# Edge attention over degree-sorted node tiles: the 53-node tile goes first and its free lanes take edges of the fullest nodes

## The chip, the core and the metric

The kernel runs on one core of a Trainium2 chip. Times are device microseconds of one execution, the median of several runs. A profile is one further execution, recorded instruction by instruction; its span runs from the first to the last instruction of the program. The core has engines with queues of their own: PE (matrix products and transposes, PEld its weight loads), DVE (element-wise work and reductions), ACT (functions and copies), POOL (here mostly the issue of indirect transfers) and SP (the issue of plain transfers).

## The reference

A graph of N = 3125 nodes with 256 features and E = 100000 edges, sorted by target, passes through two layers. The parts that the change touches are three passes of attention over edges: two transformer convolutions in layer 0 (4 heads of 64) and one attention with edge features in layer 1 (8 heads of 32).

```python
# layer 0, twice
qi, kj, vj = (q[dst], k[src], v[src])
alpha = jnp.sum(qi * kj, axis=-1) / math.sqrt(out_ch)
amax = jax.lax.stop_gradient(jax.ops.segment_max(alpha, dst, num_segments=n))
ex = jnp.exp(alpha - amax[dst])
denom = jax.ops.segment_sum(ex, dst, num_segments=n)
alpha = ex / denom[dst]
out = jax.ops.segment_sum(vj * alpha[..., None], dst, num_segments=n)
...
return out + x @ ws + bs
# layer 1
e = (edge_attr @ We.T).reshape(-1, HEADS, OUT_CH)
k_e = k[src] + e
v_e = v[src] + e
alpha = jnp.einsum('ehc,ehc->eh', q[dst], k_e) / jnp.sqrt(jnp.float32(OUT_CH))
...
```

In layer 1 alpha goes through the same softmax over the edges of a target, the weights multiply v_e, the products are summed per target, and a skip term x @ Wskip is added.

A convolution is followed by a batch norm over the nodes and a leaky ReLU. Beside them layer 0 has four blocks of a linear-attention mixer over all nodes and a routed feed-forward (16 experts, 2 per node); layer 1 has a second mixer and a feed-forward over selected nodes. The results are added to x.

## The kernel before

**Tiles of nodes.** node_order (L729) sorts the nodes by in-degree on the chip. From the sorted targets it finds each node's first edge and its number of edges, ranks the nodes by falling degree, and puts rank r into tile r // 128, lane r % 128. There are 25 tiles; 24 are full, and the last one holds the 53 nodes of least degree, with 75 lanes free. SLOTS (L715) gives each tile a fixed number of slots, one per edge of a lane: 64 for the first, then 43, 41 and so on down to 22; the sum is 833. Of the order, `perm` holds the node of a lane (free lanes get row numbers past the table's end), `near` the same limited to N - 1, `base` the lane's first edge, `lo` and `hi` the slots that hold real edges, and `some` whether the lane has any. If a tile's nodes have more edges than slots, a flag (`over`) makes the program run a general version after this one. With the reference's inputs the fullest node has 55 edges.

**Slots and steps.** `fill` (L915) gathers the source nodes of a tile's slots and makes a bias of 0 or -BIG per slot. `steps` (L1031) cuts a tile's slots into subs of at most 8 and puts two subs into a step: 64 slots are four steps of 8 + 8, 43 are 8 + 7, 7 + 7, 7 + 7, and 22 are 8 + 7 and 7. All tiles have 63 steps in a pass.

**One step.** SlotOrder (L1052) issues for each slot one indirect transfer (L723, called from L1081) that brings 128 rows of 2 KB, key and value of the source node of each lane. Then come, for each sub, the multiply of keys by q (L1103) and the sum over a head (L1106); for the step, bias and maximum (L1116 to L1120), exponential (L1131) and its sum (L1138); for each sub the multiply of values (L1144) and the sum over slots by transposes that accumulate on PE (L216). ACT takes the sum out (L1163), PE turns it back (L230), and ACT keeps it as one part of `res` (`kept`, L1171). In layer 1, EdgeOrder (L1288) adds the projected edge features to keys and values first: a transfer of the lane's edge attributes, transposes (L1320), products (L1336), and adds on DVE (L1347).

**Joining the parts.** A tile has two to four parts, one a step, each with a maximum `mx`, a sum `den` and a result `res`. `join_max` (M in PATTERN, L1049 and L1292) runs in the tile's last step and turns the maxima into factors; `join_sum` (N) into shares; `join` (J, L1202, multiply at L1206) runs in the first step of the next tile and scales `res` in place; `output` (O, U) adds the parts up on PE (L1594 or L2834), adds the skip term, and stores the tile. The tiles of mx, den and res come from pools with two buffers.

**The order of work.** PATTERN is the order in which the pieces of a step are issued to PE, DVE and ACT; these three queues follow the program (manual_schedule). At each `m` in it, a share of another stage's work is put in: the four mixer blocks of layer 0 during the two convolutions (Filling, L940), the mixer of layer 1 during the third pass (Mixing, L997). The share is the total of that work by the number of points, which counts the steps (L1537, L2851). The order on POOL and SP is not written out; the framework's scheduler sets it, and both work in order. The buffers of the gathered rows are four subs, so POOL can be one step ahead.

**Between passes.** `stages(i)` brings the tile's node features (from a table by `near` in the first convolution and in layer 1, from the stored `hsp` in the second, L1558), turns them and makes q. `output` of a convolution also takes the batch statistics of the tile's real nodes (L1614). After each convolution the stored tiles are normalised, multiplied or turned, and written by `perm` to the rows of a table (put_rows, L1038).

Of the kernel before, what the change touches and what calls it, by code (L numbers as in the profile page):

```python
# [10 lines left out]
F32 = mybir.dt.float32  # L11
# [3 lines left out]
ALU = mybir.AluOpType  # L15
AX = mybir.AxisListType
# [3 lines left out]
P = 125  # L20
# [661 lines left out]
def l0_gnn(k, x, conv, y_mix, xcur):  # L682
# [31 lines left out]

SLOTS = [  # L715
    64, 43, 41, 39, 38, 37, 36, 35, 35, 34, 33, 33, 32, 32, 31, 30, 30, 29, 29, 28, 27, 26, 25, 24, 22
# [12 lines left out]
def node_order(k, dram, src, dst, keep, tmp, pp, over, loads, weights):  # L729
# [5 lines left out]
    NQ, NB = len(SLOTS), max(SLOTS)  # L735
    assert N <= NQ * 128
# [113 lines left out]
    count = nc.vector.tensor_reduce(rank, pos, axis=AX.X, op=ALU.add)  # L850
# [18 lines left out]
    for c, t in enumerate((node[:, :NT], first[:, :NT], num)):  # L869
# [8 lines left out]
    own = one.tile([128, NQ], F32, name="own")  # L878
    nc.gpsimd.memset(past, 0.0)
    nc.gpsimd.iota(  # L880
        own, pattern=[[128, NQ]], base=0, channel_multiplier=1, allow_small_or_imprecise_dtypes=True
    )
    nc.vector.scalar_tensor_tensor(past[:, :, 0], own, N - 0.5, own, op0=ALU.is_gt, op1=ALU.mult)
    caps = one.tile([128, NQ], F32, name="caps")
    for i in range(NQ):
        nc.gpsimd.memset(caps[:, i : i + 1], float(SLOTS[i]))
    ps = pp.tile([128, 512], F32, name="cps", tag="cps")
# [12 lines left out]

    bf = one.tile([128, NQ], F32, name="bf")
# [3 lines left out]
    nc.vector.tensor_copy(perm, pl[:, :, 0])  # L905
    nc.vector.tensor_scalar_min(near, pl[:, :, 0], N - 1.0)
# [3 lines left out]
    nc.vector.tensor_tensor(more, pl[:, :, 2], caps, op=ALU.is_gt)  # L910
# [141 lines left out]
class SlotOrder:  # L1052
# [32 lines left out]
    def tile(self, i):  # L1085

        H = self.HEADS
        if i not in self.tiles:
            self.tiles[i] = dict(
                mx=self.wp.tile([128, 4, H], F32, name="mx", tag="mx"),  # L1090
                den=self.wp.tile([128, 4, H], F32, name="den", tag="den"),
                res=self.wp.tile([128, 4, D], F32, name="res", tag="res"),
            )
        return self.tiles[i]

# [73 lines left out]
    def kept(self, n):  # L1169
        t = self.steps[n]  # L1170
        self.k.nc.scalar.copy(self.tile(t["i"])["res"][:, t["c"]], t["acc"][:, D:])  # L1171


    def join_max(self, i):
        nc, H, t = self.k.nc, self.HEADS, self.tiles[i]
        n = t["n"] = len(steps(SLOTS[i]))
        mx = t["mx"]
        t["top"] = top = self.wp.tile([128, H], F32, name="top", tag="top")
        nc.vector.tensor_reduce(
            top, mx[:, :n].rearrange("p c h -> p h c"), axis=AX.X, op=ALU.max  # L1180
        )
        nc.vector.tensor_tensor(
            mx[:, :n], mx[:, :n], top.unsqueeze(1).to_broadcast([128, n, H]), op=ALU.subtract
        )
        table(self.k, EXPS)
        nc.scalar.activation(mx[:, :n], mx[:, :n], AF.Exp, scale=self.SCALE)

    def join_sum(self, i):
        nc, H, t = self.k.nc, self.HEADS, self.tiles[i]
        n, mx, den, top = t["n"], t["mx"], t["den"], t["top"]  # L1190
        nc.vector.tensor_tensor(den[:, :n], den[:, :n], mx[:, :n], op=ALU.mult)
# [96 lines left out]
class EdgeOrder(SlotOrder):  # L1288
# [69 lines left out]
    def join_sum(self, i):  # L1358
        nc, H, t = self.k.nc, self.HEADS, self.tiles[i]
        n, mx, den, top = t["n"], t["mx"], t["den"], t["top"]  # L1360
        nc.vector.tensor_tensor(den[:, :n], den[:, :n], mx[:, :n], op=ALU.mult)
# [128 lines left out]
def l0_gnn_slots(k, dram, order, a, y, pp, pq, cw, filling, tmp, first):  # L1490
# [47 lines left out]
    with k.tc.manual_schedule(engines=ORDERED):  # L1538
# [3 lines left out]
        for n in (1, 2):  # L1542
# [4 lines left out]
            with ExitStack() as st:  # L1547
                gp, wp = pl(st, ("c_kv", 4), ("c_wk", 2))

                def stages(i):  # L1550
                    o = {}

                    def load():
                        o["x"] = x = wp.tile([128, 2, 128], F32, name="xg", tag="xg")
                        if n == 1:
                            gather(k, x.rearrange("p c n -> p (c n)"), ytab, order.near[:, i : i + 1])
                        else:
                            nc.sync.dma_start(x, prev[:, i])  # L1558
# [26 lines left out]
                def output(i, res, nC):  # L1585
# [20 lines left out]
                    def put():  # L1606
# [6 lines left out]
                        for c in range(2):  # L1613
                            nc.vector.bn_stats(bst[:, c, i], t[:, c, : min(128, N - i * 128)])  # L1614
# [2257 lines left out]
```

## Time and profile before

| | us |
|---|---|
| median of 3 runs | 5158.41 (5157.67 to 5163.05) |
| profiled execution | 5147.6 |
| its span | 5145.7 |
| order of the nodes, first tables | 0 to 180 of the span |
| first convolution pass | 180 to 1370 |
| second convolution pass | 1420 to 2640 |
| routed feed-forward, tables of layer 1 | 2700 to 3340 |
| edge attention pass | 3340 to 4900 |
| last feed-forward | 4900 to 5146 |

The stages are read from the timeline, to the nearest 10 us or so. How to read the lines further down: a group is a line of the program, the engine, the operation, what it writes and from what, the shape and the number of instructions; then the busy time, the mean duration of one in nanoseconds, and the idle time of the engine just before them with what ended most of it. "issue" is idle time that ended without any wait that the profile shows. A row of the timeline gives start and duration in us, and in brackets the idle time before and its releaser. A row of windows gives the stretch, its length, and for each engine the busy time and number of instructions; then the granted PE clock, the share of the transfer engines that was busy, and GB/s. For transfers issued on POOL the trace gives the time from issue to landing, for those of SP it does not.

### The profile page before, as it was taken

To read this page: it belongs to the slowest core of one execution; us is meant where nothing else is said; L and a number is where in the kernel's file an instruction comes from. 1 tells how busy PE (TensorE), PEld (TensorE's weight loads), DVE (VectorE), ACT (ScalarE), POOL (GpSimd) and SP (SyncE) were. 2 spreads that over 40 slices of the span, in tenths; PEclk is the share of its full clock that TensorE was granted. 3 is DMA by queue.
4 is the path that set the end of the run, shared out by engine and by line. 5 is a ranking of instruction groups with operands and counts; after the bars stand their busy time and mean duration, and the time that the engine had idled before them with its cause. 6 is when DMAs were issued, how large, how long until landed. Compare 5 with 4: busy or idle time off the path is not lost. (4 is left out here: it accounts for less than half of the span.)

```text
span 5145.7 us, 55197 instructions
## 1 busy us (share of the span) xinstructions
PE 4019.3 (78%) x19111; PEld 2670.0 (52%) x19111; DVE 3905.3 (76%) x5888; ACT 1730.0 (34%) x3661; POOL 3076.1 (60%) x2946
## 2 busy tenths in 40 slices
PE   4677987688867898768963895878888987888778
PEld 2455665466645666546642562345445554544445
DVE  5698888788768888888954116299879888888956
ACT  2333344323433344433331112333333432333231
POOL 4666776577466676657745104267767767777720
PEclk8888998799987999889975997888888888888889
DMA  4576776577556677667764434445656555655610
GB/s 134 162 213 199 220 218 183 181 217 216 179 180 201 207 225 215 183 181 225 220 206 131 143 109 154 157 144 172 190 165 186 173 161 172 179 175 172 184 50 26
DMA packets 366022, 901.31 MB, mean 175 GB/s; under 512 B 90061, under 2 KB 162098, under 8 KB 365608
## 3 DMA queue, kind: packets, MB, share of 16 engines
q0 software_dynamic: 232032, 722.71, 47.9%
q1 hardware_dynamic: 125203, 158.64, 9.4%
q10 hardware_dynamic: 8499, 16.33, 0.8%
q8 instruction: 154, 2.52, 0.2%
q14 instruction: 134, 1.10, 0.1%
HBM read 806.06 MB, written 91.25 MB: 174 GB/s over the span
## 5 line engine op out<-in xcount | busy, mean ns | idle before, releaser
L723 POOL DMA_INDIRECT kv<-kvtab,slots x2499 | 2585.6, 1035 | 1093.7 <-issue 662.1
L1106 DVE TENSOR_REDUCE al<-kv 128x28 f32<-128x1792 f32 (+5 forms) x345 | 719.2, 2085 | 11.8
L216 PEld LDWEIGHTS cps<-ident,kv 128*128 128x128 f32 x4998 | 616.0, 152 | 150.9 <-issue 84.4
L216 PE MATMUL cps<-ident,kv 128*128 128x128 f32 x4998 | 664.9, 289 | 16.6 <-DVE kv L1144 10.6
L1347 DVE TENSOR_TENSOR kv<-kv,e 128x1024 f32<-128x1024 f32 x460 | 489.4, 1113 | 144.1 <-PE e L1336 65.9
L1103 DVE TENSOR_TENSOR kv<-kv,qa 128x1792 f32<-128x1792 f32 (+2 forms) x230 | 478.8, 2082 | 123.8 <-DMA kv<-kvtab,slots 93.4
L1144 DVE TENSOR_TENSOR kv<-kv,qa 128x1792 f32<-128x1792 f32 (+2 forms) x230 | 475.1, 2075 | 0.0
L2057 PE MATMUL mm<-w,hid 128*125 128x256 f32 x1600 | 386.0, 391 | 9.0 <-ACT hid L2047 9.0
L2038 PE MATMUL mm<-hTm,w 128*128 128x500 f32 (+1 forms) x896 | 375.4, 561 | 16.1 <-DVE xcur L2015 4.3
L2057 PEld LDWEIGHTS mm<-w,hid 128*125 128x125 f32 x1600 | 298.1, 194 | 59.8 <-ACT hid L2047 12.1
L146 ACT ACT_TABLE_LOAD x248 | 318.2, 1283 | 18.5 <-issue 14.2
L1336 PE MATMUL e<-we,eaT 64*128 64x256 f32 x1666 | 285.5, 444 | 34.7 <-ACT eaT L1326 25.8
L1336 PEld LDWEIGHTS e<-we,eaT 64*128 64x128 f32 x1666 | 169.3, 206 | 175.5 <-ACT eaT L1326 59.7
L1103 DVE TENSOR_TENSOR kv<-kv,q 128x1792 f32<-128x1792 f32 (+2 forms) x115 | 239.5, 2082 | 1.4
L1131 ACT ACTIVATE qa<-al 128x56 f32<-128x56 f32 (+7 forms) x126 | 27.5, 218 | 631.9 <-DVE al L1120 499.6
L1144 DVE TENSOR_TENSOR kv<-kv,al 128x1792 f32<-128x1792 f32 (+2 forms) x115 | 239.4, 2081 | 0.0
L2038 PEld LDWEIGHTS mm<-hTm,w 128*128 128x128 f32 x896 | 158.2, 197 | 153.0 <-issue 124.0
L723 POOL DMA_INDIRECT g<-ys,sloti x50 | 62.9, 1258 | 270.9 <-issue 234.1
L230 PE MATMUL cps<-ident,accT 128*128 128x128 f32 x378 | 87.4, 318 | 173.9 <-ACT accT L1163 173.8
L205 PE MATMUL mm<-wqv,hTm 128*125 128x512 f32 x400 | 195.5, 626 | 0.0
L3233 PE MATMUL w<-sel,x 32*125 32x496 f32 x400 | 144.3, 687 | 43.8 <-ACT sq L3242 33.7
L2396 DVE TENSOR_TENSOR ye<-o,b 128x256 f32<-128x256 f32 x64 | 27.2, 425 | 196.6 <-PE o L2392 196.6
(431 smaller groups left out, 7132.5 us busy)
## 6 DMA issues: line engine op xcount, KB each, us to landing
kv<-kvtab,slots POOLq DMA_INDIRECT x2499, 3.7
w<-in_L_ffn_w_dram SPq DMA_DIRECT2D x32, 512.0 KB
kvtab<-st SPq DMA_DIRECT2D x12, 1000.0 KB
qd<-qT SPq DMA_DIRECT2D x24, 500.0 KB
qT<-qd SPq DMA_DIRECT2D x24, 500.0 KB
xTg<-xcols SPq DMA_DIRECT2D x24, 500.0 KB
w<-in_L_mix_W_dram SPq DMA_DIRECT2D x8, 1024.0 KB
xs<-zero SPq DMA_DIRECT2D x16, 512.0 KB
```

What stands on the lines that cost most here:

```text
L146: k.nc.scalar.preload_act_table_set(name)
L205: nc.tensor.matmul(ps, lhs(c), w(c), start=(c == 0), stop=(bias is None and c == n_chunks - 1))
L216: m = nc.tensor.matmul(ps[:, ch], src[:, ch], k.ident, start=(start and c == 0), stop=stop, is_transpose=True, skip_group_check=True,)
L723: return k.nc.gpsimd.indirect_dma_start(out=out, out_offset=None, in_=table, in_offset=bass.IndirectOffsetOnAxis(ap=index, axis=0),)
L1103: nc.vector.tensor_tensor(kv[:, :m, :D], kv[:, :m, :D], q.unsqueeze(1).to_broadcast([128, m, D]), op=ALU.mult)
L1106: nc.vector.tensor_reduce(t["al"][:, b0 : b0 + m], self.heads(kv[:, :m, :D]), axis=AX.X, op=ALU.add)
L1144: nc.vector.tensor_tensor(v, v, t["w"][:, b0 : b0 + m].unsqueeze(3).to_broadcast([128, m, H, D // H]), op=ALU.mult)
L1336: self.k.nc.tensor.matmul(e[:, j % 2 * 2 + j // 2], eaT[r, j // 2], self.we[r], start=True, stop=True)
L1347: self.k.nc.vector.tensor_tensor(to, to, e[:, 2 * odd : 2 * odd + n].unsqueeze(2).to_broadcast([128, n, 2, D]), op=ALU.add,)
L2038: nc.tensor.matmul(ps[:, :w_], W["w1"][:, c, j * 128 : j * 128 + 128], o["hT"][:, c, :w_], start=(c == 0), stop=(c == 1),)
L2057: nc.tensor.matmul(ps[:P, :D], s["hid"][:, c, j * P : j * P + P], W["w2"][:, c, :], start=(c == 0), stop=False,)
L3233: nc.tensor.matmul(ps[:P, :496], o["x"][rows, tk], sel[rows], start=True, stop=True, tile_position=((h0 + b) * 32, 0),)
```

## The change

The sparse tile, 53 nodes and 22 slots, becomes tile 0, and the other tiles move up by one. The tile with the fullest nodes becomes tile 1 and has 45 slots where it had 64. Lane 53 + j of tile 0 (j from 0 to 74) works for node j of tile 1: it holds that node's features and its edges from the 46th on, up to 22. A lane whose node has no such edges has only slots with bias -BIG.

In node_order, the rank is shifted by 128, the last 53 ranks go to tile 0, and a product with a shifted identity brings node, first edge + 45 and edges beyond 45 from tile 1's lanes to tile 0's. `perm` is taken before this, so rows of free lanes still go past the table's end.

In a pass, tile 0's two parts are lent to tile 1: `lend` sends lanes 53 to 127 of mx, den and res by SP to lanes 0 to 74 of parts 3 and 4 of tile 1, which a memset has prepared. mx and den are copied to a small tile before, res is sent as it is. Tile 1 then joins five parts. The tiles have five parts in place of four. join_sum stands in SlotOrder and again in EdgeOrder, and both get the same two lines. The batch statistics and the second convolution's loads of tile 0 follow the new layout.

```diff
@@ SLOTS @@
-    64, 43, 41, 39, 38, 37, 36, 35, 35, 34, 33, 33, 32, 32, 31, 30, 30, 29, 29, 28, 27, 26, 25, 24, 22
+    22, 45, 43, 41, 39, 38, 37, 36, 35, 35, 34, 33, 33, 32, 32, 31, 30, 30, 29, 29, 28, 27, 26, 25, 24
@@ node_order @@
-    count = nc.vector.tensor_reduce(rank, pos, axis=AX.X, op=ALU.add)
+    nc.vector.tensor_reduce(rank, pos, axis=AX.X, op=ALU.add)
+    back = one.tile([P, NT], F32, name="back")
+    nc.vector.tensor_scalar(
+        back, rank, N - R - 0.5, -128.0 * NQ, op0=ALU.is_gt, op1=ALU.mult
+    )
+    count = nc.vector.scalar_tensor_tensor(rank, rank, 128.0, back, op0=ALU.add, op1=ALU.add)
...
+    shift = one.tile([128, 128], F32, name="shift")
+    nc.vector.memset(shift[:, :R], 0.0)
+    nc.vector.tensor_copy(shift[:, R:], k.ident[:, : 128 - R])
...
+    nc.vector.tensor_copy(perm, pl[:, :, 0])
+    nc.vector.tensor_tensor(pl[:, 0], pl[:, 0], past[:, 0], op=ALU.subtract)
+    rest = one.tile([128, 3], F32, name="beyond")
+    nc.vector.tensor_copy(rest[:, 0:1], pl[:, 1, 0:1])
+    nc.vector.tensor_scalar(rest[:, 1:2], pl[:, 1, 1:2], float(SLOTS[1]), None, op0=ALU.add)
+    nc.vector.tensor_scalar(
+        rest[:, 2:3], pl[:, 1, 2:3], -float(SLOTS[1]), 0.0, op0=ALU.add, op1=ALU.max
+    )
+    ps = pp.tile([128, 512], F32, name="cps", tag="cps")
+    nc.tensor.matmul(ps[:, 0:3], shift, rest, start=True, stop=True)
+    nc.vector.tensor_tensor(pl[:, 0], pl[:, 0], ps[:, 0:3], op=ALU.add)
...
@@ SlotOrder @@
-                mx=self.wp.tile([128, 4, H], F32, name="mx", tag="mx"),
-                den=self.wp.tile([128, 4, H], F32, name="den", tag="den"),
-                res=self.wp.tile([128, 4, D], F32, name="res", tag="res"),
+                mx=self.wp.tile([128, 5, H], F32, name="mx", tag="mx"),
+                den=self.wp.tile([128, 5, H], F32, name="den", tag="den"),
+                res=self.wp.tile([128, 5, D], F32, name="res", tag="res"),
             )
+            if i == 0:
+                self.lent = self.wp.tile([128, 2, 2 * H], F32, name="lent", tag="lent", bufs=1)
+            if i == 1:
+                t = self.tiles[1]
+                for name, a in (("mx", -BIG), ("den", 0.0), ("res", 0.0)):
+                    self.k.nc.vector.memset(t[name][:, len(steps(SLOTS[1])) : 5], a)
         return self.tiles[i]
+
+    def lend(self, name, src, lo=0):
+
+        V, c0 = 128 - self.k.N % 128, len(steps(SLOTS[1]))
+        if name != "res":
+            part = self.lent[:, :, lo : lo + self.HEADS]
+            self.k.nc.vector.tensor_copy(part, src)
+            src = part
+        self.k.nc.sync.dma_start(self.tile(1)[name][:V, c0 : c0 + 2], src[128 - V :])
...
     def kept(self, n):
         t = self.steps[n]
-        self.k.nc.scalar.copy(self.tile(t["i"])["res"][:, t["c"]], t["acc"][:, D:])
+        res = self.tile(t["i"])["res"]
+        self.k.nc.scalar.copy(res[:, t["c"]], t["acc"][:, D:])
+        if t["i"] == 0 and t["last"]:
+            self.lend("res", res[:, :2])
...
     def join_max(self, i):
         nc, H, t = self.k.nc, self.HEADS, self.tiles[i]
-        n = t["n"] = len(steps(SLOTS[i]))
+        n = t["n"] = len(steps(SLOTS[i])) + 2 * (i == 1)
         mx = t["mx"]
+        if i == 0:
+            self.lend("mx", mx[:, :2])
...
     def join_sum(self, i):
         nc, H, t = self.k.nc, self.HEADS, self.tiles[i]
         n, mx, den, top = t["n"], t["mx"], t["den"], t["top"]
+        if i == 0:
+            self.lend("den", den[:, :2], H)
...
@@ l0_gnn_slots @@
+                        elif i == 0:
+                            R = N % 128
+                            nc.sync.dma_start(x[:, :, :R], prev[:, 0, :, :R])
+                            nc.sync.dma_start(x[:, :, R:], prev[:, 1, :, : 128 - R])
                         else:
                             nc.sync.dma_start(x, prev[:, i])
...
-                            nc.vector.bn_stats(bst[:, c, i], t[:, c, : min(128, N - i * 128)])
+                            nc.vector.bn_stats(bst[:, c, i], t[:, c, : N % 128 if i == 0 else 128])
```

More of the change, by code (lines that the diff above doesn't have):

```diff
@@ L734, in node_order @@
     total = sum(SLOTS)
-    NQ, NB = len(SLOTS), max(SLOTS)
-    assert N <= NQ * 128
+    NQ, NB = len(SLOTS), 64
+    R = N % 128
+    assert N == (NQ - 1) * 128 + R and 0 < R and SLOTS[0] + SLOTS[1] > NB
     perm = keep.tile([128, NQ], I32, name="perm")
@@ L877, in node_order @@
     past = one.tile([128, NQ, 3], F32, name="past")
-    own = one.tile([128, NQ], F32, name="own")
+    own = one.tile([128, 1], F32, name="own")
     nc.gpsimd.memset(past, 0.0)
     nc.gpsimd.iota(
-        own, pattern=[[128, NQ]], base=0, channel_multiplier=1, allow_small_or_imprecise_dtypes=True
+        own, pattern=[[0, 1]], base=N - R, channel_multiplier=1, allow_small_or_imprecise_dtypes=True
     )
-    nc.vector.scalar_tensor_tensor(past[:, :, 0], own, N - 0.5, own, op0=ALU.is_gt, op1=ALU.mult)
+    nc.vector.scalar_tensor_tensor(past[:, 0, 0:1], own, N - 0.5, own, op0=ALU.is_gt, op1=ALU.mult)
+    shift = one.tile([128, 128], F32, name="shift")
+    nc.vector.memset(shift[:, :R], 0.0)
+    nc.vector.tensor_copy(shift[:, R:], k.ident[:, : 128 - R])
     caps = one.tile([128, NQ], F32, name="caps")
@@ L886, in node_order @@
         nc.gpsimd.memset(caps[:, i : i + 1], float(SLOTS[i]))
+    lim = one.tile([128, NQ], F32, name="lim")
+    nc.vector.tensor_copy(lim, caps)
+    nc.vector.memset(lim[: 128 - R, 1:2], float(SLOTS[0] + SLOTS[1]))
     ps = pp.tile([128, 512], F32, name="cps", tag="cps")
@@ L904, in node_order @@
     nc.vector.tensor_copy(base, bf)
-    nc.vector.tensor_copy(perm, pl[:, :, 0])
-    nc.vector.tensor_scalar_min(near, pl[:, :, 0], N - 1.0)
+    nc.vector.tensor_copy(near, pl[:, :, 0])
     nc.vector.tensor_tensor(lo, pl[:, :, 1], bf, op=ALU.subtract)
@@ L909, in node_order @@
     more = one.tile([128, NQ], F32, name="more")
-    nc.vector.tensor_tensor(more, pl[:, :, 2], caps, op=ALU.is_gt)
+    nc.vector.tensor_tensor(more, pl[:, :, 2], lim, op=ALU.is_gt)
     nc.vector.tensor_reduce(over[:, 1:2], more, axis=AX.X, op=ALU.max)
@@ L1360, in join_sum @@
         n, mx, den, top = t["n"], t["mx"], t["den"], t["top"]
+        if i == 0:
+            self.lend("den", den[:, :2], H)
         nc.vector.tensor_tensor(den[:, :n], den[:, :n], mx[:, :n], op=ALU.mult)
@@ L1556, in load @@
                             gather(k, x.rearrange("p c n -> p (c n)"), ytab, order.near[:, i : i + 1])
+                        elif i == 0:
+                            R = N % 128
+                            nc.sync.dma_start(x[:, :, :R], prev[:, 0, :, :R])
+                            nc.sync.dma_start(x[:, :, R:], prev[:, 1, :, : 128 - R])
                         else:
```

## The prediction

> **What bounds the kernel now.** I began with the page's groups, because the change takes nineteen slots out of every pass over the edges and the groups give the price of a slot.
>
> ```profile
> PE 4019.3 (78%) x19111; PEld 2670.0 (52%) x19111; DVE 3905.3 (76%) x5888; ACT 1730.0 (34%) x3661; POOL 3076.1 (60%) x2946
> ...
> L723 POOL DMA_INDIRECT kv<-kvtab,slots x2499 | 2585.6, 1035 | 1093.7 <-issue 662.1
> L1106 DVE TENSOR_REDUCE al<-kv 128x28 f32<-128x1792 f32 (+5 forms) x345 | 719.2, 2085 | 11.8
> ...
> L216 PE MATMUL cps<-ident,kv 128*128 128x128 f32 x4998 | 664.9, 289 | 16.6 <-DVE kv L1144 10.6
> ```
>
> 2499 gathers are 3 x 833 slots: three passes, two convolutions of layer 0 and the edge attention of layer 1. The gathers' idle time ended by "issue" is the thing to see: POOL loses time between gathers that nothing else explains. Next the table of windows, the three passes first and then two stretches of the 64-slot tile (columns: length, busy of PE, PEld, DVE, ACT, POOL, granted clock, DMA share, GB/s).
>
> ```profile
> 180.00:1370.00 1190.00, 941.07 (x4577) 690.83 (x4578) 1001.86 (x1433) 429.30 (x889) 815.96 (x858) 0.88 0.68 203
> ...
> 1420.00:2640.00 1220.00, 973.67 (x4622) 703.09 (x4621) 1014.79 (x1433) 457.89 (x958) 807.79 (x851) 0.89 0.68 202
> ...
> 3340.00:4900.00 1560.00, 1268.48 (x6852) 776.96 (x6852) 1373.60 (x1463) 532.51 (x1233) 1112.47 (x908) 0.85 0.58 172
> ...
> 1472.00:1577.00 105.00, 63.33 (x287) 44.38 (x287) 90.46 (x110) 32.24 (x75) 77.23 (x82) 0.76 0.73 214
> 3340.00:3461.00 121.00, 92.52 (x521) 58.24 (x522) 114.38 (x108) 36.06 (x75) 81.08 (x58) 0.84 0.46 135
> ```
>
> DVE is the busiest everywhere (84%, 83%, 88%), POOL looks relaxed (69%, 66%, 71%). The timeline of POOL corrects this:
>
> ```profile
> 1545.95 0.95 POOL L723 DMA_INDIRECT kv<-kvtab,slots  x1 [0.30 <-issue]
> 1547.20 0.95 POOL L723 DMA_INDIRECT kv<-kvtab,slots  x1 [0.30 <-issue]
> 1548.45 0.95 POOL L723 DMA_INDIRECT kv<-kvtab,slots  x1 [0.30 <-issue]
> ```
>
> One gather starts every 1.25 us though its bar is 0.95 long. In the convolution's first tile 82 instructions x 1.25 = 102.5 us of 105: POOL paces it. Over the whole pass 858 x 1.25 = 1072 of 1190, still more than DVE. In layer 1 DVE has 114.4 of 121 us in the first tile, so there DVE paces.
>
> **A rule against this reading.** The Trainium skill, Perfetto Trace Analysis, section Identifying the Most-Contended Engine, takes the engine with the highest occupancy; here that is DVE in all passes. The same page, section GPSIMD Engine Instruction, advises timing POOL by start-to-start spacing, and the 1.25 us above shows what that changes. By occupancy alone each convolution would gain 17 us in place of 22 below, and the total would be -51, not -61.
>
> **What is removed.** Sum of slots 833 becomes 814, steps 63 become 62: the 64-slot tile (four steps, eight subs of 8) turns into 45 (three steps, subs 8 8 8 7 7 7). The 22-slot tile is unchanged but stands first. Per convolution:
> - POOL: 19 gathers x 1.25 = 23.75 us.
> - DVE: K multiply, K reduce and V multiply last 2.285 us on a sub of 8 and 2.016 on a sub of 7. 8 x 3 x 2.285 = 54.8 becomes 9 x 2.285 + 9 x 2.016 = 38.7; with the missing step's softmax (0.22 + 0.27 + 0.22 + 0.2) 17.0 us.
> - PE: 38 transposes x 0.289 and one turn back, 11.6 us.
> - I take 22: the first tile is POOL-paced and the pass nearly so, hence three quarters of 23.75 and one quarter of 17.0. Ends: 11.6 (PE), and the elapsed rate of the tile itself. From its first mx reduction to the next tile's (197.8 to 299.7, 1490.2 to 1577.1) 64 slots took 101.9 and 86.9 us; x 19/64 that is 30 and 26.
>
> Layer 1: the same 17.0 on DVE, plus the edge adds. Eight subs of 8 are 32 adds x 1.214 = 38.9; after, 12 x 1.214 + 3 x (3 x 1.214 + 0.68) = 27.5; so 11.4 more, together 28.4. POOL: 20 gathers (one of edge attributes too) x 1.25 = 25. PE: 38 x 0.289 + 38 x 0.444 = 28. I take DVE's price with a little of its idle time, 29; the ends are 25 and 106.7 x 19/64 = 32.
>
> Two convolutions and layer 1: -22 - 22 - 29 = -73.
>
> **What is added, and where it lies.**
> (1) The lent result. join(0) multiplies res in place, so after the change it must wait until the new SP transfer of res (75 lanes, 2 KB each) has read it. Before, it ran at once:
>
> ```profile
> 300.65 2.28 DVE L1144 TENSOR_TENSOR kv<-kv,qa 128x2048 f32<-128x2048 f32 x1
> ...
> 302.05 0.37 ACT L1171 COPY res<-cps 128x256 f32<-128x256 f32 x1 [0.53 <-PE cps L230]
> ...
> 302.84 1.21 DVE L1206 TENSOR_TENSOR res<-res,qa 128x1024 f32<-128x1024 f32 x1
> ```
>
> The copy ends 0.42 us before the join. No landing of an SP transfer is in the trace; POOL's are the nearest, the kv gathers of 256 KB (least, median, most) and, in the list of issues, the row writes:
>
> ```profile
> DMA to landing us min/median/max: 3.2/3.7/10.6
> ```
>
> ```profile
> kvtab<-kvrow,perm POOLq DMA_INDIRECT x25, 2.7
> ```
>
> So the wait is 2.3 (2.7 - 0.42) to 10.2; I take 3.7 - 0.42 = 3.3 per convolution. In layer 1 the copy ends 3.3 us before the join (at 3458.57, the join at 3461.90), 0.4 is left. Sum +7, ends +5 and +28. Behind the join on DVE stand the second V multiply and the next tile's keys; PE's output transposes (L1594) wait for it, and later POOL's gathers for the buffers.
>
> [...]
>
> (2) The lent mx and den: two small DVE copies and two SP transfers a stage. They read a copy, so nothing waits for their reading; tile 1 needs mx at its last step and writes its own den some 10 us (next keys 4 x 2.29) after den is sent. Cover: tile 1's key work; without it the 3.7 us of a landing each.
> (3) DVE a stage: three memsets (at most 0.68, the 128x512 join, and 2 x 0.17), two copies 2 x 0.2, join of tile 1 over five parts where the full tile had four (+0.27): 1.7 us, x 3 = +5. PE gets one part more, two transposes, 0.6, inside its 20% idle.
> (4) node_order: two ops on rank (0.45 with their dependence), some seven ops of 0.1 to 0.2 on pl, a 128x128 product with its round trip (1.2): about 3 us later for the first slots gather. The cover is
>
> ```profile
> 167.72 0.94 POOL L723 DMA_INDIRECT xg<-ytab,near  x1 [6.52 <-PE mm L1795]
> ```
>
> POOL idles 6.5 us after the slots gathers, before anything of the first tile can start; I count 0, and +3 if that cover is gone.
> (5) Moved: the sparse tile's xg and slots gathers, 22 kv gathers, stores of hsp and row writes are issued in other places of the same POOL and SP queues, in the same number. A pass now ends with a 24-slot tile: its last step has 8 slots for 7, at most 1 us of uncovered tail. The second convolution loads tile 0 in two SP transfers for one, before its kv gathers have landed: 0.
> (6) The mixing work does not shrink; its rate per step rises by 1.6%, so it fills the same idle time in 62 steps.
>
> Sum: -73 + 7 + 5 = -61. The profiled execution has a span of 5145.7 and took 5147.6; that gives 5086.6. The median of the runs shown is 5158.4, 10.8 above it (0.2%); I carry the difference to the median: 5097.
>
> **Rivals.** About 0.2% (10 us) is what a measurement here can tell from no change.
> - A, the sum, 5097: POOL paces the convolutions, DVE layer 1. 5080 to 5115 with the ends of (1). Chance 0.58.
> - B, PE with its mixing products paces the passes (it is 79 to 81% busy and mixing stays): 11.6 + 11.6 + 28 - 16 of additions = -35, 5123. Against it: POOL and DVE waits are the long ones in the first tile. 0.18.
> - C, idle time of the removed step goes too: -30 - 26 - 32 + 12 = -76, 5082. The elapsed rate speaks for it; against it, that rate contains mixing that is only moved. 0.11.
> - D, slower: SP works in order, and a lent transfer holds what is behind it until tile 0's result is copied; if weights or q blocks of the mixing stand there and PE needs them at once, a stage loses up to one step, 20 to 25 us, three times. It decides beyond 73 - 5 = 68 us in all, 23 a stage; a little over that, 5172. In the trace SP has few issues near the join. 0.08.
> - E, the change does nothing: gathers and adds are hidden because the passes end when mixing does, 5158. Or the overflow check fires and the general program runs as well, thousands of us; but in the reference's inputs the fullest node has 55 edges and 34 nodes exceed 45, all among the 75 that can lend, so it doesn't. 0.05.
>
> Faster is A, B, C: 0.87; same 0.05; slower 0.08. The range 5070 to 5140 takes in B, C and A's ends and leaves out D and E and a little of B.
>
> **What would show it.** Gathers 2442, steps 186; the first two tiles (67 slots) as long as the first tile's 102 and 87 us plus at most 8; convolution passes 20 to 25 us shorter, layer 1 26 to 32; one DVE wait of 2 to 5 us before the first join of each convolution, released by a DMA; first kv gather still near 169. Wrong would be: a pass that keeps its length with PE's idle time gone (B, E), SP issues bunched behind the lent transfers (D), or a first kv gather later by more than 3 us.

## The result, and the profile after

The changed kernel takes 5189.56 us in the median (5181.03 to 5196.78) beside 5158.41 (5151.85 to 5173.75) for the kernel before on the same chip: a ratio of 1.0053, with a 95% interval of 1.0038 to 1.0068. It is 31 us slower; 61 us less had been predicted. The profiled execution has a span of 5190.0 us (5145.7 before).

The page of the changed kernel, its busy times and the three groups that answer to those shown of before:

```profile
PE 4004.1 (77%) x18953; PEld 2665.4 (51%) x18953; DVE 3848.0 (74%) x5875; ACT 1730.0 (33%) x3653; POOL 3001.4 (58%) x2888
...
L725 POOL DMA_INDIRECT kv<-kvtab,slots x2442 | 2524.3, 1034 | 1163.6 <-issue 650.5
L1145 DVE TENSOR_REDUCE al<-kv 128x28 f32<-128x1792 f32 (+5 forms) x339 | 703.1, 2074 | 11.6
...
L216 PE MATMUL cps<-ident,kv 128*128 128x128 f32 x4884 | 643.5, 288 | 15.0 <-DVE kv L1183 9.8
```

The work went as predicted: 57 gathers fewer, POOL 75 us less busy, DVE 57, PE 15. But the gathers' idle time grew by 69.9 us (1093.7 before). All of the saving, and more, came back as waiting.

To find where, the passes are cut at rows that both kernels have: the maximum of a step (`mx<-al`, L1119 before, L1158 after), namely the first of the pass, the first of the 43-slot tile and the last of the 24-slot tile; and at the end of a convolution the aggregation of its statistics (`bmv<-bst`). Worked out from the starts of these rows, after minus before in us:

| | conv. 1 | conv. 2 | layer 1 | sum |
|---|---|---|---|---|
| first block: 64 slots before, 22 + 45 after | +20.1 | +17.5 | +18.5 | +56.1 |
| tiles of 43 to 24 slots, the same in both | +16.8 | +23.7 | +40.1 | +80.6 |
| from there to the end (in layer 1 of the program) | -26.5 | -33.6 | -37.6 | -97.7 |
| up to the first block, and between passes | | | | +5.3 |

The rows add up to the 44 us between the two profiled executions; the medians are 31 apart, since the profiled execution of before lies 11 us under its median. The first and third rows are what the change moves: -42 us together, against the -61 planned. The second row should be zero: 23 tiles with the same slots, steps and order. Windows of that middle stretch, in the kernel before (length; busy PE, PEld, DVE, ACT, POOL; clock; DMA share; GB/s):

```profile
299.71:1337.20 1037.49, 845.23 (x4079) 616.88 (x4080) 884.25 (x1277) 382.37 (x784) 714.13 (x753) 0.89 0.69 206
1577.13:2601.95 1024.82, 840.93 (x4038) 612.73 (x4039) 878.43 (x1236) 392.64 (x807) 694.95 (x732) 0.90 0.70 207
3461.30:4852.66 1391.36, 1147.81 (x6193) 699.10 (x6192) 1219.14 (x1306) 489.59 (x1134) 1011.96 (x834) 0.86 0.59 175
```

and in the changed kernel:

```profile
319.87:1374.20 1054.33, 850.28 (x4150) 631.01 (x4151) 880.67 (x1264) 386.03 (x783) 704.42 (x742) 0.88 0.68 200
1602.81:2651.32 1048.51, 843.70 (x4106) 624.71 (x4107) 873.26 (x1227) 395.62 (x805) 687.99 (x725) 0.89 0.68 201
3503.07:4934.54 1431.47, 1153.35 (x6156) 703.06 (x6156) 1218.81 (x1302) 483.99 (x1125) 994.24 (x824) 0.85 0.58 170
```

DVE and POOL do slightly less in it, PE has up to 0.6% more, and the stretch is 1.6%, 2.3% and 2.9% longer. By the Trainium skill, Perfetto Trace Analysis, section Identifying the Most-Contended Engine, one looks at the engine with the highest occupancy. Here that is DVE, and its occupancy fell (85.2% to 83.5% in the first stretch): the longer time is nobody's work. What differs is PE's instruction count, 4079 and 4150: the mixing pieces that are dealt out between the steps are not the same ones in this stretch.

The waits of the second convolution's stretch say how that acts. Before:

```profile
POOL kv L723 <- PE cps L216: 82.7, 22, 17.3
...
DVE kv L1103 <- DMA kv<-kvtab,slots: 26.4, 22, 4.2
...
PE cps L230 <- ACT accT L1163: 70.0, 30, 7.1
PE mm L1726 <- ACT xh L1716: 35.7, 41, 8.4
```

After:

```profile
POOL kv L725 <- PE cps L216: 93.3, 26, 9.8
POOL kv L725 <- DVE kv L1183: 14.8, 3, 14.2
...
DVE kv L1142 <- DMA kv<-kvtab,slots: 55.1, 30, 9.7
...
PE cps L230 <- ACT accT L1202: 83.2, 26, 10.2
PE mm L1778 <- ACT xh L1768: 46.7, 24, 9.1
```

(Engine, instruction, what it waited for: us in total, times, longest.) PE waits longer for ACT, partly in the mixing (the layer norm's `xh`); POOL waits longer for buffers that the transposes at L216 release; DVE waits 29 us longer for the gathered rows, more than the 23.7 by which the stretch grew.

One place shows it at the scale of instructions: the first step of the 34-slot tile in the second convolution, 17.8 us long before (1984.32 to 2002.16) and 25.3 after (2031.76 to 2057.01). The timeline of PE before:

```profile
1986.31 1.89 PE L2057 MATMUL mm<-w,hid 128*125 128x256 f32 x8
1988.03 1.69 PE L216 MATMUL cps<-ident,kv 128*128 128x128 f32 x14
```

and after, PE and then POOL:

```profile
2034.34 2.78 PE L1778 MATMUL mm<-ident,xh 125*128 125x125 f32 x8 [6.00 <-ACT xh L1768]
2036.91 0.64 PE L230 MATMUL cps<-ident,accT 128*128 128x128 f32 x2
2037.34 4.88 PE L1847 MATMUL mm<-hTm,wk 128*128 128x500 f32 x8
2042.05 1.69 PE L216 MATMUL cps<-ident,kv 128*128 128x128 f32 x14
...
2044.02 0.94 POOL L725 DMA_INDIRECT kv<-kvtab,slots  x1 [6.99 <-DVE kmx L1858]
```

Before, this step met a plain product of the mixer; the slot transposes came 3.7 us after the step's maximum. After, it meets the beginning of a mixer block, whose layer norm goes through DVE and ACT. PE, in order, sits 6.0 us in front of it, the slot transposes come 10.3 us after the maximum and end at 2043.74, and only then is a buffer free: POOL stood 7 us (the row that it names ended at the same time). In the kernel before the same piece stands in the next step, behind the slot transposes (timeline of PE):

```profile
2009.34 1.69 PE L216 MATMUL cps<-ident,kv 128*128 128x128 f32 x14
2013.53 0.33 PE L1726 MATMUL mm<-ident,xh 125*128 125x125 f32 x1 [2.50 <-ACT xh L1716]
```

There PE waits 2.5 us for it, and POOL's gathers go on, one per 1.25 us. This is one place of many: that next step is 5.0 us shorter after the change (13.7 for 18.7), and over the stretch single steps differ by -18 to +17 us. What is left over is the +23.7.

### The profile page after: what moved, and what is told of

It reads as the page before. It is cut to its first block, busy times and chain, and to the rows that moved or that the text cites. A ratio compares the mean times of both kernels' runs of the same rounds, so it can differ in the third digit from the quotient of the medians.

```text
span 5190.0 us, 54756 instructions
## 1 busy us (share of the span) xinstructions
PE 4004.1 (77%) x18953; PEld 2665.4 (51%) x18953; DVE 3848.0 (74%) x5875; ACT 1730.0 (33%) x3653; POOL 3001.4 (58%) x2888
## 5 line engine op out<-in xcount | busy, mean ns | idle before, releaser
L725 POOL DMA_INDIRECT kv<-kvtab,slots x2442 | 2524.3, 1034 | 1163.6 <-issue 650.5
L1145 DVE TENSOR_REDUCE al<-kv 128x28 f32<-128x1792 f32 (+5 forms) x339 | 703.1, 2074 | 11.6
L216 PEld LDWEIGHTS cps<-ident,kv 128*128 128x128 f32 x4884 | 594.0, 150 | 144.5 <-issue 82.4
L216 PE MATMUL cps<-ident,kv 128*128 128x128 f32 x4884 | 643.5, 288 | 15.0 <-DVE kv L1183 9.8
L1393 DVE TENSOR_TENSOR kv<-kv,e 128x1024 f32<-128x1024 f32 x452 | 478.4, 1108 | 174.2 <-PE e L1382 78.9
L1142 DVE TENSOR_TENSOR kv<-kv,qa 128x1792 f32<-128x1792 f32 (+2 forms) x226 | 468.0, 2071 | 165.7 <-DMA kv<-kvtab,slots 136.9
L1183 DVE TENSOR_TENSOR kv<-kv,qa 128x1792 f32<-128x1792 f32 (+2 forms) x226 | 464.5, 2065 | 0.0
L2109 PE MATMUL mm<-w,hid 128*125 128x256 f32 x1600 | 401.3, 401 | 23.9 <-ACT hid L2099 23.8
L2090 PE MATMUL mm<-hTm,w 128*128 128x500 f32 (+1 forms) x896 | 361.2, 546 | 7.8 <-DVE xcur L2117 5.1
L1170 ACT ACTIVATE qa<-al 128x56 f32<-128x56 f32 (+5 forms) x124 | 27.0, 217 | 575.3 <-DVE al L1159 359.8
L1778 PE MATMUL mm<-ident,xh 125*128 125x125 f32 x400 | 98.4, 345 | 109.2 <-ACT xh L1768 95.7
```

Source lines behind the costliest of these rows:

```text
L216: m = nc.tensor.matmul(ps[:, ch], src[:, ch], k.ident, start=(start and c == 0), stop=stop, is_transpose=True, skip_group_check=True,)
L725: return k.nc.gpsimd.indirect_dma_start(out=out, out_offset=None, in_=table, in_offset=bass.IndirectOffsetOnAxis(ap=index, axis=0),)
L1142: nc.vector.tensor_tensor(kv[:, :m, :D], kv[:, :m, :D], q.unsqueeze(1).to_broadcast([128, m, D]), op=ALU.mult)
L1145: nc.vector.tensor_reduce(t["al"][:, b0 : b0 + m], self.heads(kv[:, :m, :D]), axis=AX.X, op=ALU.add)
L1183: nc.vector.tensor_tensor(v, v, t["w"][:, b0 : b0 + m].unsqueeze(3).to_broadcast([128, m, H, D // H]), op=ALU.mult)
L1393: self.k.nc.vector.tensor_tensor(to, to, e[:, 2 * odd : 2 * odd + n].unsqueeze(2).to_broadcast([128, n, 2, D]), op=ALU.add,)
```

## The experiments

Most of the experiments ran on chips like that of the two traces (kernel before 5157.5 to 5160.4 us). Those marked "other chip" ran on two slower ones: the first four experiments on one where it takes 5596, the four further down on one where it takes 5657. A ratio is always to the kernel before on the same chip, in runs beside it.

**The cut, the order and the lending apart** (other chip). `cut_only` is the kernel before with 45 slots for its first tile, and leaves out the edges beyond the 45th:

```diff
-    64, 43, 41, ...
+    45, 43, 41, ...
-    nc.vector.tensor_tensor(more, pl[:, :, 2], caps, op=ALU.is_gt)
+    nc.vector.tensor_scalar(more, pl[:, :, 2], 64.5, None, op0=ALU.is_gt)
```

> The kernel before with 45 slots for its first tile and nothing else: sparse tile still last, nothing lent. It leaves out the edges beyond the 45th of 34 nodes. Theory S (the price of a slot was right, the order and the lending ate it): -73 us in all, so about 5085, each convolution pass 20 to 24 shorter, layer 1 about 29. Rival M (the passes don't run at the pace of a slot; the mixing work and its place against the steps set it): 5125 to 5165, idle time of DVE up by most of what its busy time lost.

`first_only` is the changed kernel with the light tile first, but 64 slots behind it and nothing lent:

```diff
-    22, 45, 43, 41, ...
+    22, 64, 43, 41, ...
```

> The changed kernel with 64 slots in tile 1 and nothing lent: only the order of tiles is new, slots and steps are those of before. Theory O (the short two-step tile at the start costs): 5190 to 5230, most of it in the first two tiles of a pass. Theory L (lending costs): 5150 to 5165. Rival M: anything within some 30 us of before, with the difference spread over all tiles of a pass and not at its start.

`after_nolend` is the changed kernel without the memsets, the lending and the fifth part (the lent edges are left out), `after_rate63` the changed kernel with the mixing rate of 63 steps:

```diff
-        n = t["n"] = len(steps(SLOTS[i])) + 2 * (i == 1)
+        n = t["n"] = len(steps(SLOTS[i]))
```

> The changed kernel without the lending: no memsets, no transfers, three parts in tile 1. It leaves out the edges beyond the 45th of 34 nodes. Theory L: at or below 5120, since the lending would hold the whole loss. By the trace of after the waits for the sent result are 6.0 and 4.7 us in the convolutions and nothing in layer 1, so without L: 5170 to 5185.

```diff
-            mix.restart(len(first) - 2.5)
+            mix.restart(len(first) - 1.5)
```

> The changed kernel with the mixing spread over 63 steps in place of 62, the rate per step of the kernel before. Rival M: moves by more than 10 us one way or the other, since another alignment of mixing and steps results. Theories O and L: 5185 to 5200, no more than the mixing that is left for the end of a stage.

| | ratio | 95% |
|---|---|---|
| cut_only | 0.9931 | 0.9893 to 0.9969 |
| first_only | 1.0226 | 1.0145 to 1.0306 |
| after_nolend | 0.9993 | 0.9953 to 1.0033 |
| after_rate63 | 1.0000 | 0.9969 to 1.0031 |

The cut gains 40 us there, about half of theory S's 73. The light tile in front loses, by more than theory O said, even with no slot saved and nothing lent. With the old rate of mixing (the new one is 1.6% higher) the changed kernel still gains nothing; the changed kernel itself did not run on this chip, so what the rate is worth can't be told. What it is about the front was open.

**The same two kernels without mixing, and the pair at the other end.** The mixers of both layers are left out of `before_nomix` and `after_nomix`:

```diff
-    ... lambda n: Filling(pieces, n) ...
+    ... lambda n: Filling([], n) ...
-                begin.mixing = Mixing(pieces, 1)
+                begin.mixing = Mixing([], 1)
```

> The kernel before, with the mixing work that fills the slot passes of both layers left out (the two layer mixers are not computed, so the output lacks their share). It is the base for the next run. Both theories: PE's load in the three passes falls, the two convolutions go at the pace of POOL's gathers (about 1.25 us each: 783 slots x 1.25 = 979 us and the joins, against 1192 and 1163 us now), layer 1 at DVE's (close to 1560 us of 1826). In all some 400 to 600 us under the kernel before.

> The changed kernel with the same mixing work left out. Theory M (the gain of the smaller tile is eaten by the mixing work, which comes with every step and now meets other tiles): without it the cut shows whole, 50 to 75 us under the run above, each pass 15 to 30 us shorter. Theory O (the order itself costs: a pass that begins with the light tile pays at its start and in its hand-over, whatever fills it): the two runs are within 20 us of each other, and the first 67 slots of a pass still take 10 us or more longer than the 64 slots before.

> The changed kernel unchanged, as the anchor of this call. Both theories: 1.004 to 1.007 of the kernel before, if this chip is like the first one; nearer to 1.00 to 1.01 if it is like the one of the last call.

`late_pair` puts the light tile next to last and the fullest tile last; ranks, lanes, loads and lending follow (PS is the light tile's number):

```diff
-    22, 45, 43, 41, ... 25, 24
+    43, 41, ... 25, 24, 22, 45
+PS = len(SLOTS) - 2
...
-        back, rank, N - R - 0.5, -128.0 * NQ, op0=ALU.is_gt, op1=ALU.mult
+        back, rank, 127.5, 128.0 * NQ, op0=ALU.is_lt, op1=ALU.mult
-    count = nc.vector.scalar_tensor_tensor(rank, rank, 128.0, back, op0=ALU.add, op1=ALU.add)
+    count = nc.vector.scalar_tensor_tensor(rank, rank, -128.0, back, op0=ALU.add, op1=ALU.add)
...
-        if i == 0:
+        if i == PS:
             self.lend("mx", mx[:, :2])
```

> The same idea with the pair of tiles at the end of a pass: 43, 41, ... 24, then the nearly empty tile of 22 slots and last the fullest tile of 45, which gets the lent partial sums; nothing is left out. Theory O: the passes begin with full tiles again, so the cost of the early light tile is gone and the cut is kept but for a join at the end that waits for its lent result: 25 to 50 us under the kernel before (ratio 0.990 to 0.995). Theory M: the mixing still meets other tiles than before, and a smaller tile's steps still carry as much of it: within 15 us of the changed kernel, not under 1.000.

| | median, us | ratio | 95% |
|---|---|---|---|
| before_nomix | 4774.55 | 0.9247 | 0.9226 to 0.9267 |
| after_nomix | 4707.11 | 0.9119 | 0.9102 to 0.9136 |
| after_again | 5185.43 | 1.0050 | 1.0036 to 1.0064 |
| late_pair | 5091.97 | 0.9865 | 0.9844 to 0.9885 |

Without mixing the change is worth 67 us, as theory M said (the kernel before gets 386 us faster without it, a little less than the 400 to 600 expected). The middle stretch of the second convolution, windows of before_nomix and then of after_nomix:

```profile
1436.49:2353.66 917.17, 359.15 (x2002) 321.47 (x2002) 730.38 (x777) 85.56 (x282) 693.63 (x735) 0.68 0.72 216
```

```profile
1423.75:2340.70 916.95, 363.00 (x2004) 324.94 (x2004) 729.93 (x777) 84.65 (x280) 687.13 (x727) 0.67 0.72 215
```

The same to 0.2 us (in the first convolution 946.5 and 942.1, in layer 1 1286.9 and 1279.9). So it is the mixing that makes these tiles longer. But late_pair carries all of the mixing, has the same 814 slots and 62 steps and the same lending, and is 68 us faster than before, more than even theory O's 25 to 50. So "the mixing eats a smaller tile's gain" does not hold either, and each of the two theories is half refuted: it must be how order and mixing meet.

**Exchanging the mixing plans.** A piece of mixing is put in at fixed points of each step. In the kernel before, four steps' worth has been dealt out when the 43-slot tile begins; after, five. `after_phase` is the changed kernel with the old plan: the rate of 63 steps, nothing in the first step of a pass, and the share of two steps behind the last step of a convolution (where the kernel before has the two steps of its last tile). `before_phase` is the kernel before with the new plan. Both are complete.

```diff
 after_phase, SlotOrder and EdgeOrder
-                m=(True, lambda: mix(3 / PATTERN.count("m"))),
+                m=(n > 0, lambda: mix(3 / PATTERN.count("m"))),
...
+        for _ in range(2 * PATTERN.count("m")):
+            mix(3 / PATTERN.count("m"))
         n = len(self.steps) - 1
 before_phase
-                m=(True, lambda: mix(3 / PATTERN.count("m"))),
+                m=(i < NQ - 1, lambda: mix((6 if n == 0 else 3) / PATTERN.count("m"))),
```

They ran on the second of the other chips first:

> The changed kernel, its mixing work dealt out so that each of the tiles from 43 to 24 slots meets the same mixing pieces as in the kernel before: the rate of 63 steps, none in the first step of a pass, and two steps' worth more behind the last step of a convolution. Nothing is left out. Theory P (it is the position of the mixing pieces against the steps that costs): these tiles go back to the times of before, within 8 us a pass (they stand at +19, +24 and +30 to 40 us), the first 67 slots lose another 5 to 10 us each, the two steps' worth behind the convolutions cost up to 17 us each: 5085 to 5130 us. Theory Q (the order costs in itself once PE is loaded: the light first tile leaves the pipeline of gathers behind for the rest of the pass): the tiles stay 15 us or more a pass over before, and the time at 5160 or more.

> The counterpart: the kernel before, its mixing work dealt out so that these tiles meet the pieces that they meet in the changed kernel (the rate of 62 steps, a double helping in the first step of a pass, none in the two steps of the last tile). Nothing is left out. Theory P: the tiles from 43 to 24 slots take on the extra 19, 24 and 30 to 40 us of the changed kernel, and the time is 40 to 85 us over before. Theory Q: they stay within 8 us of before, and the time within 25 us.

There they took 0.9994 (0.9971 to 1.0017) and 1.0065 (1.0034 to 1.0096) of the kernel before: in the direction of theory P, but smaller than it said, and with no profile of the two unchanged kernels on that chip to lay them beside. Between these two, the stretch with the old plan is 6 us longer in the first convolution, 10 shorter in the second and 29 shorter in layer 1. And after_rate63, whose second convolution holds the old plan's pieces (4036 instructions of PE), is there 6 us longer than after_nolend with the new plan's (4102). So on the slower chips the plan's effect is not everywhere of one sign. Then on a chip like the first:

> The changed kernel with the mixing pieces where the kernel before has them (none in the first step of a pass, two steps' worth behind the last step of a convolution). On a chip like that of the first traces (kernel before near 5160 us): theory P: the tiles from 43 to 24 slots within 8 us a pass of the kernel before (the changed kernel stands at +19, +24 and +30 to 40), the time 5085 to 5130 us. Theory Q: 15 us or more a pass over before, the time at 5160 or more.

> The kernel before with the mixing pieces where the changed kernel has them. Theory P: the same tiles 15 to 40 us a pass over before, the time 5200 to 5245 us. Theory Q: within 8 us a pass, the time within 25 us of before. On the other chip it took 1.0065 of the kernel before, between the two.

after_phase2 took 5138.02 us, 0.9960 (0.9946 to 0.9975); before_phase2 5223.65, 1.0136 (1.0110 to 1.0163). The middle stretch, windows of after_phase2 and of before_phase2:

```profile
318.68:1352.47 1033.79, 846.38 (x4080) 618.25 (x4081) 883.84 (x1274) 382.23 (x783) 703.70 (x742) 0.89 0.68 205
1595.43:2617.73 1022.30, 838.24 (x4036) 611.61 (x4037) 877.23 (x1235) 392.17 (x805) 686.32 (x723) 0.90 0.69 206
3463.02:4863.10 1400.08, 1155.83 (x6193) 702.41 (x6192) 1219.91 (x1306) 489.84 (x1133) 999.54 (x823) 0.85 0.58 172
```

```profile
299.12:1351.99 1052.87, 849.47 (x4150) 629.84 (x4151) 881.33 (x1266) 385.43 (x784) 712.88 (x751) 0.88 0.68 202
1597.74:2643.47 1045.73, 843.11 (x4109) 621.32 (x4110) 873.83 (x1229) 396.33 (x808) 698.17 (x739) 0.89 0.69 205
3506.43:4926.02 1419.59, 1141.32 (x6168) 697.28 (x6168) 1218.38 (x1301) 483.94 (x1126) 1006.26 (x834) 0.86 0.58 173
```

The times change sides with the plan. Middle stretch against the kernel before, in us (the +19, +24 and +30 to 40 of the expectations are an earlier reading of the first row):

| | conv. 1 | conv. 2 | layer 1 |
|---|---|---|---|
| after, both profiles | +16.8, +16.0 | +23.7, +23.3 | +40.1, +29.7 |
| after_phase2 (old plan) | -3.7 | -2.5 | +8.7 |
| before_phase2 (new plan) | +15.4 | +20.9 | +28.2 |

The two profiles of the changed kernel show the scatter: under 1 us in the convolutions, 10 in layer 1. PE's instruction counts say that the stretch holds the same pieces (in the first convolution 4080 with the old plan, 4150 with the new; in layer 1 6193 and 6156, where before_phase2 has 6168). The waits follow: in the second convolution DVE's wait for gathered rows is, in after_phase2 and then in before_phase2,

```profile
DVE kv L1142 <- DMA kv<-kvtab,slots: 27.9, 20, 5.1
```

```profile
DVE kv L1103 <- DMA kv<-kvtab,slots: 51.7, 29, 9.1
```

against 26.4 before and 55.1 after. Theory Q is refuted on this chip: with the old plan the light first tile leaves nothing behind beyond the scatter. That after_phase2 as a whole is 41 us over the predicted 5097, and 8 over theory P's 5130, is mostly the plan's own price: the mixing behind the last step of a convolution, and in the last step of layer 1, is uncovered, and from the last maximum on the three passes are 19.6, 14.3 and 16.8 us longer than in the changed kernel. By the same reading first_only moved the plan by two steps (six steps' worth before the 43-slot tile) and cut_only by one the other way; that was not exchanged there.

**Mixing by slots instead of by steps.** If steps of 7 slots suffer because they get as much mixing as steps of 16, a share by slots should help:

```diff
+            next_ = sum(self.steps[min(n + 1, len(self.steps) - 1)]["subs"]) * len(self.steps) / sum(SLOTS)
...
-                m=(True, lambda: mix(3 / PATTERN.count("m"))),
+                m=(True, lambda: mix(3 / PATTERN.count("m") * next_)),
```

> The changed kernel with each step's share of mixing in proportion to the slots of the step that is gathered meanwhile (7 to 16), instead of the same for every step. Nothing is left out. Theory P, if the loss is that short steps get as much mixing as long ones: 30 to 80 us under the changed kernel. Theory Q: within 20 us of it.

> The kernel with the pair of tiles at the end of a pass (22 slots, then 45), with the mixing in proportion to the slots as in the run above. Theory P: 10 to 60 us under the kernel with the pair at the end (5092 us beside a kernel before of 5160), the best of all. Theory Q: within 15 us of it, since there the light tile does not come first.

> The kernel with the light tile and the fullest tile at the end of a pass, and the mixing in proportion to the slots gathered meanwhile. Theory P: 10 to 50 us under the kernel with the pair at the end and even mixing (0.9865 of the kernel before): 0.977 to 0.985. Theory Q: 0.984 to 0.990, as the even one. On the other chip it took 0.9864.

On the other chip after_byslots took 0.9890 (0.9830 to 0.9951), late_byslots 0.9864 (0.9807 to 0.9922). On a chip like the first late_byslots2 took 0.9926 (0.9901 to 0.9950), slower than the 0.9865 of late_pair and outside the ranges of both theories. In late_pair it is no improvement: it is one more position, and a worse one. For the changed kernel it ran only on the other chip, where after_phase, with steps of equal share in another position, took 0.9994. The changed kernel itself did not run there, so even filling and position are not told apart.

**The price of the lending.** after_nolend again, on a chip like the first:

> The changed kernel with nothing lent (the edges beyond the 45th of the fullest nodes are left out; no transfers, no fills, four parts). If lending costs what the prediction put (7 us of wait and 5 us of DVE work): 8 to 20 us under the changed kernel, nearly all of it in the first 67 slots of a pass, and the tiles from 43 to 24 slots as in the changed kernel (P and Q alike, since neither has lending in it). A third theory, L (the lending delays the first joins and with them the whole pass): 40 us or more under the changed kernel, with these tiles back at the times of before.

5158.84 us, 1.0005 (0.9993 to 1.0017), beside 1.0050 with lending: some 23 us, somewhat more than expected. The middle stretches keep their excess (+14.8, +22.8, +26.9), so theory L falls. Against the second profile of the changed kernel, the first block of the convolutions is 4.4 and 3.7 us shorter and that of layer 1 the same; another 6 us lie between the second convolution and layer 1, where nothing is lent and where profiles of different kernels scatter from 700 to 715. About 8 us can be placed, the rest can't.

**Is late_pair's gain its order or its position?** The mixing of late_pair one step later (none in the first step) and one step earlier (a double helping in it), the rate set so that all of it is still dealt out:

```diff
 late_minus
-                m=(True, lambda: mix(3 / PATTERN.count("m"))),
+                m=(n > 0, lambda: mix(3 / PATTERN.count("m"))),
 late_plus
+                m=(True, lambda: mix((6 if n == 0 else 3) / PATTERN.count("m"))),
```

> The kernel with the light tile and the fullest tile at the end of a pass (0.9865 of the kernel before), with no mixing in the first step of each pass, so that every tile meets the pieces one step later. Nothing is left out. If the position of the pieces is what counts in any order: the tiles from 43 to 24 slots move by 10 to 40 us in at least one pass, either way, and the time by more than 15 us. If the order carries the gain: within 12 us of it (0.984 to 0.989).

> The same with a double helping of mixing in the first step of each pass, so that every tile meets the pieces one step earlier. The two theories expect of it what they expect of the run above; under the first one it need not move the same way.

late_minus took 5119.13 us, 0.9928 (0.9908 to 0.9948), late_plus 5114.04, 0.9919 (0.9897 to 0.9941). One step either way costs 22 to 27 us, most of it in the second convolution, where the stretch is 1047.0 and 1045.2 us long instead of 1022.6. With the mixing by slots it was 39 us under the kernel before. So 39 to 46 us of late_pair's 68 are there in every position tried, the rest is a good position.

The fastest version found is late_pair, 68 us under the kernel before and 93 under the change. Its page:

```profile
PE 3993.7 (79%) x18953; PEld 2643.8 (52%) x18953; DVE 3840.2 (75%) x5875; ACT 1733.8 (34%) x3655; POOL 3015.7 (59%) x2888
...
L726 POOL DMA_INDIRECT kv<-kvtab,slots x2442 | 2525.3, 1034 | 1068.7 <-issue 639.6
```

The work is that of the changed kernel to 0.5%; the gathers' idle time is 95 us less.

## Why the prediction was wrong

**The step that failed** is (6): the mixing work "fills the same idle time in 62 steps". The work is the same, but its pieces are not interchangeable: one that runs through DVE and ACT (a layer norm, the start of a block) stopped PE for 6.0 us in front of a step's slot transposes and for 2.5 us behind them, where one that is a plain product had let it run on. When each piece meets another step, the idle time does not stay the same. Cost: +81 us in the middle stretches (+69 in the second profile), where the prediction had none; it is most of the miss of 92. That the plan makes it is shown by the exchange of plans, in both directions, on a chip like the first; by which steps the loss outweighs the gain was followed at one place only. The prediction looked for the effect in the rate, which changed by 1.6%; the position moved by a whole step.

**The removed work, -73.** Right where it can be read by itself: without mixing the change as a whole took 67 us off, against the sum of -61. That POOL paces the convolutions and DVE layer 1 holds there too: in before_nomix the second convolution's stretch holds 735 instructions of POOL in 917 us, one per 1.25, and in layer 1's stretch DVE is busy for 1158 of 1287 us. With mixing, neither engine's pace sets the pass, but the waits between them.

**First block, "plus at most 8".** +20, +17.5 and +18.5. Without mixing +13, +5 and +8. Part of the rest is a fifth helping of mixing, since the block has five steps for four: DVE is busy 92.0 us in the second convolution's block, in place of 79.7, PE 75.5 in place of 62.4. With four helpings (after_phase2) the block stands at +19, +12 and +9, so the fifth is worth 9 us in layer 1 and 5 in the second convolution, but 1 in the first; without lending (after_nolend2) at +16, +14 and +19. What else makes it longer in the first convolution stays open. That a pass gets its mixing by steps stood in the text; that 67 slots in five steps therefore carry a quarter more of it than 64 in four was not worked out.

**(1) The lent result, +7.** The waits are there, before the first join of each convolution, and none in layer 1 (timeline of DVE in the first convolution; waits in the second):

```profile
260.00 0.69 DVE L1252 TENSOR_TENSOR res<-res,qa 128x512 f32<-128x512 f32 x1 [6.00 <-DMA res<-res]
```

```profile
DVE res L1252 <- DMA res<-res: 4.7, 1, 4.7
```

Together 10.7 us instead of 7; 6.0 lies over the stated 2 to 5, 4.7 within. The transfer itself was sized well: from the end of ACT's copy (255.91, 1540.11) to the join it took 4.1 and 2.8 us, where 3.7 was taken from POOL's landings. The Trainium skill, DMA: Bandwidth & Descriptors, section Anatomy of one DMA, fits a transfer on the gpsimd path with 2.0 us plus its bytes at 436 GB/s: for 150 KB an estimate of 2.35 us, below both of these, which SP issued. The excess is the copy, later than in the kernel before: DVE had been idle for 1.9 us when it ended, in both convolutions.

**(2), (3) and (5).** No row shows a wait for the lent mx and den. The two copies took 0.16 to 0.23 us each. Lending as a whole costs 23 us by the medians against 12 in (1) to (3), of which 8 can be placed. The moved tile by itself, (5), shows no cost in the middle stretches, where theory Q would have put one; its part in the longer first blocks was not measured.

**(4) node_order.** The first slots gather starts 5.3 us later, not 3, but the cover held: the first kv gather is at 170.5, from 169.0.

**The rivals.** B named the mixing, but as PE's load, and still saw a gain; PE's share of the middle stretches fell from about 82% to 81%. (B's sum takes 16 us of additions where the others take 12; with 12 it gives 5119.) E let the passes end when the mixing does, so that nothing changes; with the same mixing work they became 10, 8 and 21 us longer (the columns of the first table). D, the slower one, named SP; but behind the lent transfer (issued 255.94) SP issued the next at 257.76, as soon as its source was there (`qT`, ended 257.73). The true rival, the mixing displaced against the steps, was not among them, and 87% for faster left no room for it.

## What to carry to other kernels

Where filler work is dealt out at counted points, a change of the number or order of steps moves every later piece to another place. On this kernel a step's shift was worth 0.4% to 1.4% of the time on chips like the first, as much as the change itself; a forecast of such a change should carry that as a term of either sign, and a comparison should hold the plan fixed, as after_phase does, before it judges the edit. If the edit is free in where it sits, try several positions of the filler: here the same 814 slots gave 5092 to 5190 us.

## What the runs showed of the hardware

With less work for PE the granted clock was lower: without mixing 0.716 on the mean in the kernel before, with it 0.863. The same 128x128 transposes took 327 ns instead of 289:

```profile
L216 PE MATMUL cps<-ident,kv 128*128 128x128 f32 x4998 | 791.8, 327 | 182.1 <-issue 123.1
```

The same program, after_nolend, took 5158.84 us on one chip and 5599.03 on another. The passes were 8 to 13% longer there (first convolution 1344.8 and 1193.8 us), while the last feed-forward took the same (254.7 and 255.3), and single instructions lasted the same to 2% (transposes 293 and 288 ns). What grew is idle time, in the middle stretch of the first convolution 298 us of DVE instead of 172: 64.8 us of it the profile calls "issue" instead of 6.8, and 53 us end by a releaser that it calls "remote" instead of none. What makes it, no run settled.
